# Values projected with tokens on the partitions, and score keys taken by image columns, in two attention blocks

## The chip, the cores and the metric

The kernel runs on one core of one Trainium2 chip. The metric is device time in microseconds (us): the median of several executions of the whole program. Beside it stands one profiled execution, from which every duration of a single instruction below is taken. A core has five engines that run side by side: TensorE (PE) multiplies matrices, VectorE (DVE), ScalarE (ACT) and GpSimd (POOL) work on elements, and SyncE (SP) here only issues transfers. They wait for each other through semaphores.

## What is computed

The reference applies two layers to four images of 32 x 32 tokens with 768 channels, in float32. Each layer is `x = x + attention(groupnorm(x))`, the norm having 32 groups and no weights. Cut to what matters:

```python
qkv = x @ Wqkv                      # layer 1: x @ qkv_w.T + qkv_b
q, k, v = 12 heads of 64 channels each
rel_h = einsum('bhwc,hkc->bhwk', q, Rh)   # one number per query and key row
rel_w = einsum('bhwc,wkc->bhwk', q, Rw)   # one number per query and key column
scores = scale * q @ k.T + (rel_h[..., :, None] + rel_w[..., None, :])
out = softmax(scores) @ v
return out @ Wproj + bproj
```

In layer 1 q is scaled once more in the score and once in the position terms. The softmax of a query runs over all 1024 keys, so the order in which the keys stand doesn't change it, as long as the values stand in the same order.

## The kernel before, in words

**Units.** An "image" in the code is one image in one layer, so there are 8 (`NI`), and each has 6 pairs of heads (`NP`); a pair fills 128 partitions, 64 channels for each head. There are 48 pairs, `g`. The queries of a pair come in 8 tiles of 128 (`n`). A unit is one `(g, n)`; the main loop goes through the 384 units, and an image takes its six pairs one after the other.

**Layout.** The normed input `xn` lies with channels on the partitions, in 6 tiles of 128 channels by 1024 tokens. A product with it contracts over channels.

**Projections.** `project_in(g, which, i)` computes q, k or v of a pair (`which` 0, 1, 2) for one half `i` of the tokens. For every tile of 128 channels it issues two matmuls, one for the upper and one for the lower 64 channels, each with its own PSUM bank; the two occupy different rows of the array. The weights are stationary and the tokens move, 512 at a time, so the result has channels on the partitions. The two banks are added on the way out: ACT copies the first (L234, or L236 with the bias in layer 1), DVE adds the second (L237). It is a generator with six steps of two matmuls.

**Values.** For q and k the result stays as it is. For v it is written with tokens reordered, element by element 16 bytes apart, into a temporary, and then `turn_values` (L249) transposes it on TensorE in eight 128 x 128 blocks (L254) and ACT copies it out (L255), so that tokens are on the partitions. Each of the eight blocks is a "plane" of 128 keys.

**Positions.** `positions(g, i)` multiplies half of the queries with the table of relative positions, copies the result into a temporary (L274) and writes it to HBM from ACT's queue (L276). `diagonals(g)` reads it back with slanted access patterns, 16 transfers on SP's queue (L295), into `rel`. `biases` adds the row and the column term into a tile of 128 queries by 1024 keys on POOL (L305).

**Scores.** `scores` multiplies queries and keys (L317), DVE adds the biases and finds the minimum of the negated score (L326), ACT takes the exponential and its sum (L330), and `divide` normalises on POOL (L340). The result lies with queries on the partitions.

**Turning the weights.** `turn` transposes blocks of 32 x 32 on DVE (L354), which puts the second index of a key, its column in the image, on 32 partitions. For two tiles of queries together ("a quarter") the result is written to HBM (L357) and `read_back` fetches it in such a form (L365) that each of eight planes has 128 keys on the partitions. Which keys a plane holds follows from this round trip, and the values must be stored to match. `weigh` multiplies values and planes (L380), both heads side by side in the columns of the array, and DVE copies the result out (L385).

**Output.** `project_out` multiplies with the output weights (L449) in two parts of three pairs each, adds the residual and keeps statistics for the next layer's norm. In layer 0 the statistics of the next image's input come from half chunks that are loaded for this alone (`load_stats`, tile `xs`), as only three of its six chunks (`AHEAD`) are resident at that time.

**Order.** It is written out by hand. In each unit the loop issues what earlier units deferred (the lists `early` and `later`), biases two units ahead, the scores of the next unit, then the turning of the present one, and then a share of the list `todo`, which holds the next pair's projections and four output groups. `shares = [6, 6, 0, 6, 12, 6, 0, 12]` gives the steps for n = 0 to 7. So the next pair's six projection groups are spent by n = 5; at n = 7 there follow output groups, with `turn_values` between them. `weigh` stands at n = 6 for the first two quarters and at n = 2 of the next pair for the others. Deferred work runs one or two units later. Engines take their instructions in this order, and so does each queue: a transfer whose buffer isn't free holds up all those behind it on SP. TensorE's results go to two PSUM tiles of two banks for the scores (`ps_s`) and two for everything else (`ps_m`).

Of the kernel before, what the change touches and what calls it, by code (L numbers as in the profile page):

```python
# [52 lines left out]
def attention_blocks(ctx: ExitStack, tc: tile.TileContext, a: dict, out: bass.AP):  # L55
# [3 lines left out]
    const = ctx.enter_context(tc.tile_pool(name="const", bufs=1))  # L59
    wpool = ctx.enter_context(tc.tile_pool(name="weights", bufs=3))  # L60
    wopool = ctx.enter_context(tc.tile_pool(name="wo", bufs=3))
    xpool = ctx.enter_context(tc.tile_pool(name="x", bufs=NC + AHEAD))
    apool = ctx.enter_context(tc.tile_pool(name="attn", bufs=6))
    qkpool = ctx.enter_context(tc.tile_pool(name="qk", bufs=2))
    vpool = ctx.enter_context(tc.tile_pool(name="v", bufs=2))
    scpool = ctx.enter_context(tc.tile_pool(name="sc", bufs=6))
    tmppool = ctx.enter_context(tc.tile_pool(name="tmp", bufs=2))
    tbpool = ctx.enter_context(tc.tile_pool(name="tb", bufs=3))
    ptpool = ctx.enter_context(tc.tile_pool(name="pt", bufs=2))
    relpool = ctx.enter_context(tc.tile_pool(name="rel", bufs=2))  # L70
    xspool = ctx.enter_context(tc.tile_pool(name="xs", bufs=1))
    iopool = ctx.enter_context(tc.tile_pool(name="io", bufs=4))
# [15 lines left out]

    def load_x(im, c):
        l, b = images[im]  # L90
        x = xpool.tile([P, S], FP, tag="xn", name=f"xn_{im}_{c}")
        xn_of[im].append(x)
        nc.sync.dma_start(out=x, in_=srcs[l][b][c * P : (c + 1) * P, :])

    def load_w(g, which):
        im, pair = divmod(g, NP)
        src = a[f"wqkv{images[im][0]}"][pair].rearrange("k p (c o) -> k p c o", c=NC)
        w = wpool.tile([P, NC, P], FP, tag="w", name=f"w_{g}_{which}")
        w_of[g, which] = w
        nc.sync.dma_start(out=w, in_=src[which])  # L100

# [4 lines left out]


    ident = const.tile([P, P], FP, tag="ident", name="ident")
    make_identity(nc, ident)

# [33 lines left out]
    def stats(im, c, i, x):  # L144
# [5 lines left out]
        if i == 1:  # L150
            nc.vector.bn_aggr(mv_of[im][:, c, :], st.rearrange("p i s -> p (i s)"))

    def load_stats(im, c, i):
        l, b = images[im]
        if c < AHEAD:
            x = xn_of[im][c][:, i * HALF : (i + 1) * HALF]
            later.append(lambda: stats(im, c, i, x))
            return
        x = xspool.tile([P, HALF], FP, tag="xs", name=f"xs_{im}_{c}_{i}")
        nc.sync.dma_start(out=x, in_=srcs[l][b][c * P : (c + 1) * P, i * HALF : (i + 1) * HALF])  # L160
        later.append(lambda: stats(im, c, i, x))

# [42 lines left out]

    qkv_of, v_of, rel_of, t_of = {}, {}, {}, {}

    def project_in(g, which, i):

        im, pair = divmod(g, NP)  # L210
        l = images[im][0]
        xn, w = xn_of[im], w_of[g, which]
        cols = slice(i * HALF, (i + 1) * HALF)
        if i == 0:
            pool, tag = (tmppool, "tmp") if which == 2 else (qkpool, "qk"[which])
            qkv_of[g, which] = pool.tile([P, S], FP, tag=tag, name=f"{'qkv'[which]}_{g}")
        to = qkv_of[g, which][:, cols]
        if which == 2:
            to = qkv_of[g, 2].rearrange("p (k j y) -> p y k j", y=4, k=NT)[:, 2 * i : 2 * i + 2]
        t = ps_m.tile([P, 2, HALF], FP, tag="m", name=f"pj_{g}_{which}_{i}")  # L220
        for c in range(NC):
            for a in range(2):
                rows = slice(a * D, (a + 1) * D)
                nc.tensor.matmul(  # L224
                    t[:, a, :], lhsT=w[rows, c, :], rhs=xn[c][rows, cols],
                    start=(c == 0), stop=(c == NC - 1),
                )
            if c < NC - 1:
                yield True
        t = [t[:, a, :] for a in range(2)]  # L230
        if which == 2:
            t = [x.rearrange("p (y k j) -> p y k j", y=2, k=NT) for x in t]
        if l == 0:
            nc.scalar.copy(to, t[0])  # L234
        else:
            nc.scalar.activation(to, t[0], AF.Identity, bias=bqkv[:, which, pair : pair + 1])  # L236
        nc.vector.tensor_tensor(to, t[1], to, ALU.add)  # L237
        if which == 0:
            (later if g else mid).append(lambda: positions(g, i))
        if which == 2 and i == 1:  # L240
            late.append(lambda: turn_values(g))
        if i == 1 and g + 1 < NPAIR:
            later.append(lambda: load_w(g + 1, which))
        if which == 2 and i == 1 and pair == NP - 1 and im + 1 < NI:
            for c in range(AHEAD, NC):
                load_x(im + 1, c)
        yield True

    def turn_values(g):  # L249

        v_of[g] = vpool.tile([P, NT, P], FP, tag="v", name=f"v_{g}")
        t = ps_m.tile([P, NT, P], FP, tag="m", name=f"vt_{g}")
        for k in range(NT):
            nc.tensor.transpose(t[:, k, :], qkv_of[g, 2][:, k * P : (k + 1) * P], ident)  # L254
        nc.scalar.copy(v_of[g], t)  # L255

    def positions(g, i):

        l = images[g // NP][0]
        q = qkv_of[g, 0]  # L260
        if i == 0:
# [21 lines left out]
    def diagonals(g):  # L283
        td = t_of[g]
        for h in range(2):
            for ax in range(2):
                for y in range(4):


                    at = HW * y * 2 * P + h * P + HW - 1 + 2 * HW * ax - (y if ax == 0 else 0)  # L290
                    src = bass.AP(
                        td.tensor, td.offset + at,
                        [[2 * P - ax, HW], [P * 2 * P - (4 if ax == 0 else 0), NT], [1, HW]],
                    )
                    nc.sync.dma_start(out=rel_of[g][32 * y : 32 * y + 32, h, ax, :, :], in_=src)  # L295

# [3 lines left out]
    def biases(g, n):  # L300
        rel = rel_of[g]
        for h in range(2):
            sc = scpool.tile([P, HW, HW], FP, tag="sc", name=f"sc_{g}_{n}_{h}")
            sc_of[g, n, h] = sc
            nc.gpsimd.tensor_tensor(  # L305
                sc, rel[:, h, 0, n, :].unsqueeze(2).to_broadcast([P, HW, HW]),
                rel[:, h, 1, n, :].unsqueeze(1).to_broadcast([P, HW, HW]), ALU.add,
            )

    def scores(g, n):  # L310
        q, k = qkv_of[g, 0], qkv_of[g, 1]
        ps = [ps_s.tile([P, S], FP, tag="s", name=f"s_{g}_{n}_{h}") for h in range(2)]
# [11 lines left out]
        for h in range(2):  # L324
            sc = sc_of[g, n, h].rearrange("p y x -> p (y x)")
            nc.vector.tensor_tensor_reduce(  # L326
# [8 lines left out]
    def divide(g, n):  # L335
        st = st_of[g, n]
        nc.vector.reciprocal(st[:, 2, :], st[:, 1, :])  # L337
        for h in range(2):
            sc = sc_of[g, n, h].rearrange("p y x -> p (y x)")
            nc.gpsimd.tensor_scalar(sc, sc, st[:, 2, h : h + 1], 1.0, ALU.mult, ALU.mult)  # L340
# [29 lines left out]
    def weigh(g, quarters):  # L370

        if quarters[0] == 0:
            attn_of[g] = apool.tile([P, S], FP, tag="attn", name=f"attn_{g}")
        n = len(quarters)
        av = ps_m.tile([P, S], FP, tag="m", name=f"av_{g}_{quarters[0]}")[:, : n * 2 * P]
        for at, quarter in enumerate(quarters):
# [7 lines left out]
        at = quarters[0] * 2 * P  # L384
        nc.vector.tensor_copy(  # L385
            attn_of[g][:, at : at + n * 2 * P].rearrange("p (q n r i) -> p q r n i", q=n, n=2, r=4),
            av.rearrange("p (q r n i) -> p q r n i", q=n, n=2, r=4),
        )

# [14 lines left out]
    def fetch(upto):  # L404

        while fetched[0] <= min(upto + 2, len(parts) - 1):
            im, p, o, i = parts[fetched[0]]
# [23 lines left out]
    def fetch_last():  # L431
# [3 lines left out]
        for c in range(NC // 2, NC):  # L435
            w = wpool.tile([P, NC, P], FP, tag="w", name=f"w_last_{c}")
            nc.sync.dma_start(out=w, in_=src[c])
            for o in range(NC):
                wo_of[NI - 1, o, c] = w[:, o, :]
# [37 lines left out]

    early, mid, later, late, behind, behind2 = [], [], [], [], [], []

# [4 lines left out]
    def prepare(g):  # L484
        return [(project_in(g, which, i), NC) for which in range(3) for i in range(2)]

# [4 lines left out]
    def take(groups, n):  # L491
# [8 lines left out]
        while groups and groups[0][1] == 0:  # L500
            for _ in groups.pop(0)[0]:
                pass

    with tc.manual_schedule(engines=ENGINES):
# [23 lines left out]
        for at, (g, n) in enumerate(units):  # L528
            im, pair = divmod(g, NP)
            end = im + 1 == NI  # L530
            if n == 0:
                shares = [6, 6, 0, 6, 12, 6, 0, 12]
                ins = (todo if at == 0 else []) + (prepare(g + 1) if g + 1 < NPAIR else [])
                if pair < 3:
# [7 lines left out]
                else:  # L542
                    todo = ins + put_out(im, 0, range(8, 12))
                    if end:
                        fetch_last()
                        todo += put_out(im, 1, range(12)) + put_out(im, 2, range(0, 12, 2))
                        shares = [0, 6, 6, 6, 6, 2, 0, 4]
            if pair < 3 and not end and n % 4 == 0 and 2 * pair + n // 4 < AHEAD:
                load_x(im + 1, 2 * pair + n // 4)
            if pair < 3 and im + 1 < B and n in (1, 3, 5, 6):  # L550
                c, i = divmod(4 * pair + n // 2, 2)
                load_stats(im + 1, (c + AHEAD) % NC, i)
            run(early)
# [12 lines left out]
            if n == NT - 1:  # L566
                take(todo, share // 4)
                share -= share // 4
            if late and n == NT - 1 or at == 1:
                late.pop(0)()  # L570
            turn(g, n)
# [72 lines left out]
```

## Time and profile before

| | us |
|---|---|
| median of three runs | 3561.37 (3557.85 to 3562.34) |
| the profiled execution: its time | 3557.89 |
| the profiled execution: its span, first to last instruction | 3556.0 |
| TensorE busy in the span | 3511.2 |
| VectorE busy | 2404.5 |
| GpSimd busy | 2298.1 |
| ScalarE busy | 1309.4 |
| TensorE weight loads busy (beside the products) | 1733.6 |

The transfers move 1084 MB, 305 GB/s on the mean. Busy time of an engine is time in which at least one of its instructions was running. In a row of the groups of instructions the line of the code comes first, then the engine, the operation, output and input by their names, shapes, the count, and after the bar the busy time in us and the mean duration of one in ns; last, how long the engine had been idle just before such instructions, and whose end let them go. Matmuls overlap, so their mean duration is longer than the time that one more of them costs. What one costs is read from the chain, where each piece begins as the one before it ends. A row of the stages holds the stretch, its length, and busy time and count for PE, its weight loads, DVE, ACT and POOL, then the granted TensorE clock, the share of the transfer engines and GB/s. In the list of transfers the median time from issue to landing is 6.5 us for the position products, 6.9 us for the weights and 2.1 us for each position read.

### The profile page before, as it was taken

The page shows a single profiled execution, that of the slowest core. Times are in us where ns is not written, and L with a number is a line of the kernel's source. Part 1 is how long each engine was busy: PE and PEld are TensorE (multiplying, and loading weights), DVE is VectorE, ACT ScalarE, POOL GpSimd, SP SyncE. Part 2 cuts the span into 40 slices and gives each one's busy share as a digit, 9 for nine tenths or more (in the row PEclk, how much of TensorE's full clock was granted, in tenths as well). Part 3 has the DMA queues.
Part 4 walks back from the last instruction along what each step waited for, and adds up shares of the span by engine and source line. Part 5 has one row for each costly group of instructions (what it writes and reads, how often), then busy time and mean ns, then how long its engine had stood idle before and what let it go on. Part 6 is the DMA issues. An engine that isn't in the chain of part 4 may idle for free.

```text
span 3556.0 us, 51176 instructions
## 1 busy us (share of the span) xinstructions
PE 3511.2 (99%) x19200; PEld 1733.6 (49%) x19200; DVE 2404.5 (68%) x3533; ACT 1309.4 (37%) x1992; POOL 2298.1 (65%) x1548
## 2 busy tenths in 40 slices
PE   6999999999999999999999999999999999999998
PEld 3455545454544445454444445454444445454443
DVE  3776767767677676666766667666766667666666
ACT  2444333333333333333334343333334343333331
POOL 2777666666666666666666666666666666666663
PEclk9999999999999999999999999999999999999999
DMA  3989988888988888988988888988889888888876
GB/s 126 322 310 314 327 300 323 315 311 301 328 322 309 312 305 313 321 309 287 325 318 320 308 289 321 324 317 285 314 320 327 308 289 318 315 311 281 311 278 261
DMA packets 629593, 1084.29 MB, mean 305 GB/s; under 512 B 247648, under 2 KB 310624, under 8 KB 580192
## 3 DMA queue, kind: packets, MB, share of 16 engines
q1 hardware_dynamic: 577600, 1028.58, 82.3%
q10 hardware_dynamic: 51744, 52.44, 4.2%
q8 instruction: 151, 2.47, 0.3%
q14 instruction: 98, 0.80, 0.1%
HBM read 580.59 MB, written 500.27 MB: 304 GB/s over the span
## 4 chain that ended last, share of the span: by engine, by line
PE 96%; DMA 2%; DVE 1%; POOL 1%; issue 0%; SPq 0%; ACT 0%; DVEq 0%; POOLq 0%
PE pj L224 41%; PE s L317 19%; PE av L380 19%; PE o L449 14%; PE tp L269 3%; PE vt L254 1%; DMA td<-tb 0%; DVE sc L326 0%; DVE tb L354 0%; POOL sc L305 0%; DMA w<-in_wqkv 0%; DMA xs<-in_x 0%; POOL sc L340 0%; SPq L295 0%; DMA pt<-td 0%
## 5 line engine op out<-in xcount | busy, mean ns | idle before, releaser
L340 POOL TENSOR_SCALAR sc<-sc,sm 128x1024 f32<-128x1024 f32 x768 | 851.7, 1122 | 1167.8 <-DVE sm L337 1136.1
L224 PE MATMUL pj<-xn,w 64*128 64x512 f32 x6912 | 1537.1, 591 | 27.1 <-DVE xn L199 26.0
L305 POOL TENSOR_TENSOR sc<-rel 128x1024 f32<-128x1024 f32 x768 | 1458.1, 1920 | 42.3 <-DMA rel<-tdr 42.3
L330 ACT ACTIVATE sc<-sc,sm 128x1024 f32<-128x1024 f32 x768 | 879.2, 1145 | 1427.8 <-DVE sm L326 1427.8
L326 DVE CUSTOM_DVE_ANT_0 sc<-s,sc 128x1024 f32<-128x1024 f32 x768 | 909.8, 1222 | 291.9 <-PE s L317 277.7
L224 PEld LDWEIGHTS pj<-xn,w 64*128 64x128 f32 x6912 | 674.8, 188 | 843.1 <-issue 813.3
L354 DVE STREAM_TRANSPOSE tb<-sc 128x1024 f32<-128x1024 f32 x768 | 909.4, 1222 | 3.6 <-DMA td<-tb 2.9
L317 PE MATMUL s<-k,q 64*128 64x512 f32 x3072 | 752.1, 598 | 7.4 <-DVE sm L326 7.3
L380 PE MATMUL av<-pt,v 128*64 128x256 f32 x6144 | 685.7, 381 | 2.3 <-DMA pt<-td 2.1
L380 PEld LDWEIGHTS av<-pt,v 128*64 128x64 f32 x6144 | 433.0, 137 | 284.6 <-issue 29.6
L449 PE MATMUL o<-attn,wo 128*128 128x512 f32 x1080 | 487.5, 601 | 0.0
L317 PEld LDWEIGHTS s<-k,q 64*128 64x128 f32 x3072 | 288.3, 187 | 340.7 <-issue 321.4
L449 PEld LDWEIGHTS o<-attn,wo 128*128 128x128 f32 x1080 | 197.8, 190 | 258.1 <-issue 247.3
L237 DVE TENSOR_TENSOR v<-pj,v 128x512 f32<-128x512 f32 x96 | 108.2, 1127 | 285.7 <-ACT v L234 141.4
L385 DVE COPY attn<-av 128x512 f32<-128x512 f32 (+1 forms) x97 | 66.3, 684 | 179.5 <-PE av L380 179.5
L274 ACT COPY t<-tp 128x1024 f32<-128x1024 f32 x96 | 97.2, 1012 | 216.5 <-PE tp L269 216.3
L330 ACT ACTIVATION_READ_ACCUMULATOR sc<-sc,sm 128x1 f32 x768 | 143.1, 186 | 0.0
L237 DVE TENSOR_TENSOR q<-pj,q 128x512 f32<-128x512 f32 x96 | 66.4, 692 | 109.9 <-ACT q L234 59.5
L237 DVE TENSOR_TENSOR k<-pj,k 128x512 f32<-128x512 f32 x96 | 66.2, 689 | 92.5 <-ACT k L234 46.8
L269 PEld LDWEIGHTS tp<-tab,q 64*128 64x128 f32 x1536 | 99.2, 187 | 40.6 <-issue 40.1
L460 DVE SCALAR_TENSOR_TENSOR res<-o,bo,res 128x512 f32<-128x512 f32 x84 | 62.9, 749 | 70.1 <-PE o L449 59.1
L269 PE MATMUL tp<-tab,q 64*128 64x128 f32 x1536 | 108.1, 278 | 0.0
(38 smaller groups left out, 810.1 us busy)
## 6 DMA issues: line engine op xcount, KB each, us to landing
td<-tb SPq DMA_DIRECT2D x384, 1024.0 KB, 5.6
pt<-td SPq DMA_DIRECT2D x382, 1024.0 KB, 7.8
w<-in_wqkv SPq DMA_DIRECT2D x144, 384.0 KB, 6.9
tdr<-t ACTq DMA_DIRECT2D x96, 512.0 KB, 6.5
rel<-tdr SPq DMA_DIRECT2D x768, 32.0 KB, 2.1
part<-res SPq DMA_DIRECT2D x84, 256.0 KB, 5.5
res<-part SPq DMA_DIRECT2D x84, 256.0 KB, 8.8
wo<-in_wo SPq DMA_DIRECT2D x90, 192.0 KB, 8.4
```

The costliest lines, as they stand in the source:

```text
L224: nc.tensor.matmul(t[:, a, :], lhsT=w[rows, c, :], rhs=xn[c][rows, cols], start=(c == 0), stop=(c == NC - 1),)
L237: nc.vector.tensor_tensor(to, t[1], to, ALU.add)
L269: nc.tensor.matmul(ps[:, h, j, :], lhsT=q[rows, at * P : (at + 1) * P], rhs=tabs[l][rows, :], start=True, stop=True,)
L274: nc.scalar.copy(t, ps.rearrange("p h j r -> p j h r"))
L305: nc.gpsimd.tensor_tensor(sc, rel[:, h, 0, n, :].unsqueeze(2).to_broadcast([P, HW, HW]), rel[:, h, 1, n, :].unsqueeze(1).to_broadcast([P, ...
L317: nc.tensor.matmul(ps[h][:, cols], lhsT=q[rows, n * P : (n + 1) * P], rhs=k[rows, cols], start=True, stop=True,)
L326: nc.vector.tensor_tensor_reduce(out=sc, in0=ps[h], in1=sc, scale=-scale, scalar=BIG, op0=ALU.add, op1=ALU.min, accum_out=st[:, 0, h : h + 1],
L330: nc.scalar.activation(sc, sc, AF.Exp, bias=st[:, 0, h : h + 1], scale=-1.0, accum_out=st[:, 1, h : h + 1],)
L340: nc.gpsimd.tensor_scalar(sc, sc, st[:, 2, h : h + 1], 1.0, ALU.mult, ALU.mult)
L354: nc.vector.transpose(tb[:, :, j, :], sc_of[g, n, h])
L380: nc.tensor.matmul(av[rows, at * 2 * P : (at + 1) * 2 * P], lhsT=v_of[g][:, k, rows], rhs=pt_of[g, quarter, h][:, :, k, :], start=(k == 0) ...
L449: nc.tensor.matmul(t, lhsT=wo_of[im, o, c], rhs=attn_of[im * NP + c][:, cols], start=(c == c0), stop=(c == c1 - 1),)
```

## The change

Values are projected for two pairs, that is four heads, at once by a new function `project_values`. In it the tokens are stationary and the weights move: for each plane of 128 tokens and each half tile of channels, 128 columns of `xn` are loaded into the array and 256 value channels stream through. The result has tokens on the partitions. There are no transposes of v, no temporary for it, and no identity matrix. A plane is every eighth token, so the 128 stationary columns lie 8 floats apart in `xn`.

So that planes of scores hold the same tokens, keys are stored by image columns (`k` is written in the order x, y), and the biases are added in that order. The round trip through HBM is as it was; what it puts into plane k is now every eighth token. The groups of v of two pairs are spread over both: groups 0 and 1 are issued with the first pair's q and k, groups 2 and 3 with the second's. The value bias of layer 1 is added to the weighted sum in `weigh`, since the weights of a query sum to one.

Value weights come as one transfer of 768 KB for two pairs into a single buffer of their own. The other weights have two buffers instead of three, output weights two instead of three and are fetched two parts later, the temporary one instead of two, v three instead of two. The tile `xs` is gone: for the statistics, whole chunks go through the three resident input tiles first, and the chunks that stay there are loaded a pair later. For the first pair, half of the position reads are issued by ACT.

```diff
-    wpool = ctx.enter_context(tc.tile_pool(name="weights", bufs=3))
-    wopool = ctx.enter_context(tc.tile_pool(name="wo", bufs=3))
+    wpool = ctx.enter_context(tc.tile_pool(name="weights", bufs=2))
+    wopool = ctx.enter_context(tc.tile_pool(name="wo", bufs=2))
-    vpool = ctx.enter_context(tc.tile_pool(name="v", bufs=2))
+    vpool = ctx.enter_context(tc.tile_pool(name="v", bufs=3))
-    tmppool = ctx.enter_context(tc.tile_pool(name="tmp", bufs=2))
+    tmppool = ctx.enter_context(tc.tile_pool(name="tmp", bufs=1))
-    xspool = ctx.enter_context(tc.tile_pool(name="xs", bufs=1))
...
+        if which == 2:
+            w = wpool.tile([P, NC, 2 * P], FP, tag="wv", bufs=1, name=f"wv_{g}")
+            src = a[f"wv{images[im][0]}"][pair // 2]
...
-        if which == 2:
-            to = qkv_of[g, 2].rearrange("p (k j y) -> p y k j", y=4, k=NT)[:, 2 * i : 2 * i + 2]
...
+        if which == 1:
+            to = to.rearrange("p (x y) -> p x y", x=HW)[:, :, i * HW // 2 : (i + 1) * HW // 2]
+            t = [x.rearrange("p (y x) -> p x y", x=HW) for x in t]
...
-    def turn_values(g):
-
-        v_of[g] = vpool.tile([P, NT, P], FP, tag="v", name=f"v_{g}")
-        t = ps_m.tile([P, NT, P], FP, tag="m", name=f"vt_{g}")
-        for k in range(NT):
-            nc.tensor.transpose(t[:, k, :], qkv_of[g, 2][:, k * P : (k + 1) * P], ident)
-        nc.scalar.copy(v_of[g], t)
+    def project_values(g, i):
+
+        im, pair = divmod(g, NP)
+        xn, w = xn_of[im], w_of[g, 2]
+        if i == 0:
+            for h in range(2):
+                v_of[g + h] = vpool.tile([P, NT, P], FP, tag="v", name=f"v_{g + h}")
+        t = ps_m.tile([P, 2, 2, 2 * P], FP, tag="m", name=f"pv_{g}_{i}")
+        for k in range(2):
+            for c in range(NC):
+                for a in range(2):
+                    rows = slice(a * D, (a + 1) * D)
+                    nc.tensor.matmul(
+                        t[:, a, k, :],
+                        lhsT=xn[c][rows, :].rearrange("p (m k) -> p k m", k=NT)[:, 2 * i + k, :],
+                        rhs=w[rows, c, :], start=(c == 0), stop=(c == NC - 1),
+                    )
+                if c % 2 and (k, c) != (1, NC - 1):
+                    yield True
+        for h in range(2):
+            to = v_of[g + h][:, 2 * i : 2 * i + 2, :]
+            cols = slice(h * P, (h + 1) * P)
+            nc.scalar.copy(to, t[:, 0, :, cols])
+            nc.vector.tensor_tensor(to, t[:, 1, :, cols], to, ALU.add)
+        if i == 3:
+            if g + 2 < NPAIR:
+                later.append(lambda: load_w(g + 2, 2))
+            if pair == NP - 2 and im + 1 < NI:
+                for c in range(AHEAD, NC):
+                    load_x(im + 1, c)
+        yield True
...
-                    nc.sync.dma_start(out=rel_of[g][32 * y : 32 * y + 32, h, ax, :, :], in_=src)
+                    (nc.scalar if h and not g else nc.sync).dma_start(out=rel_of[g][32 * y : 32 * y + 32, h, ax, :, :], in_=src)
...
-                sc, rel[:, h, 0, n, :].unsqueeze(2).to_broadcast([P, HW, HW]),
-                rel[:, h, 1, n, :].unsqueeze(1).to_broadcast([P, HW, HW]), ALU.add,
+                sc, rel[:, h, 1, n, :].unsqueeze(2).to_broadcast([P, HW, HW]),
+                rel[:, h, 0, n, :].unsqueeze(1).to_broadcast([P, HW, HW]), ALU.add,
...
+        if images[im][0] == 0:
+            nc.vector.tensor_copy(to, av)
+        else:
+            for q in range(n):
+                nc.vector.tensor_scalar(to[:, q], av[:, q], bqkv[:, 2, pair : pair + 1], None, ALU.add)
...
-        while fetched[0] <= min(upto + 2, len(parts) - 1):
+        while fetched[0] <= min(upto, len(parts) - 1):
...
-        return [(project_in(g, which, i), NC) for which in range(3) for i in range(2)]
+
+        todo = [(project_in(g, which, i), NC) for which in range(2) for i in range(2) if g < NPAIR]
+        if g % 2:
+            return todo + [(project_values(g - 1, i), NC) for i in (2, 3)]
+        return todo + [(project_values(g, i), NC) for i in (0, 1) if g < NPAIR]
...
+    loads = {(1, 0): 0, (1, 4): 1, (2, 0): 2}
+    loads0 = {(0, 0): 0, (0, 1): 1, (0, 4): 2}
...
-            if pair < 3 and not end and n % 4 == 0 and 2 * pair + n // 4 < AHEAD:
-                load_x(im + 1, 2 * pair + n // 4)
-            if pair < 3 and im + 1 < B and n in (1, 3, 5, 6):
-                c, i = divmod(4 * pair + n // 2, 2)
-                load_stats(im + 1, (c + AHEAD) % NC, i)
+            if (pair, n) in loads and not end:
+                load_x(im + 1, loads[pair, n])
+            if im + 1 < B:
+                if (pair, n) in loads0:
+                    load_x(im + 1, loads0[pair, n], loads0[pair, n] + AHEAD)
+                if pair < 3 and n in (1, 3, 5, 6):
+                    c, i = divmod(4 * pair + n // 2, 2)
+                    x = xn_of[im + 1][c % AHEAD][:, i * HALF : (i + 1) * HALF]
+                    later.append(lambda c=c, i=i, x=x: stats(im + 1, (c + AHEAD) % NC, i, x))
...
-            if late and n == NT - 1 or at == 1:
-                late.pop(0)()
```

## The prediction

> **What bounds the kernel.** I read the page first, then the groups kept apart by shape, the stages, and the chain that ended last within one pair of heads.
>
> ```profile
> span 3556.0 us, 51176 instructions
> ...
> PE 3511.2 (99%) x19200; PEld 1733.6 (49%) x19200; DVE 2404.5 (68%) x3533; ACT 1309.4 (37%) x1992; POOL 2298.1 (65%) x1548
> ...
> PE 96%; DMA 2%; DVE 1%; POOL 1%; issue 0%; SPq 0%; ACT 0%; DVEq 0%; POOLq 0%
> PE pj L224 41%; PE s L317 19%; PE av L380 19%; PE o L449 14%; PE tp L269 3%; PE vt L254 1%; DMA td<-tb 0%; DVE sc L326 0%; DVE tb L354 0%; POOL sc L305 0%; DMA w<-in_wqkv 0%; DMA xs<-in_x 0%; POOL sc L340 0%; SPq L295 0%; DMA pt<-td 0%
> ```
>
> TensorE is busy and is the chain; every other engine has at least 30% to spare. The stages say where this holds.
>
> ```profile
> 0.00:90.00 90.00, 60.39 (x294) 28.24 (x296) 33.44 (x61) 19.64 (x27) 27.12 (x28) 0.96 0.39 126
> 208.00:3490.00 3282.00, 3279.95 (x18054) 1624.96 (x18052) 2246.44 (x3286) 1231.00 (x1873) 2170.02 (x1452) 1.00 0.88 310
> ```
>
> From 208 to 3490 us TensorE is idle for 2.05 us (second figure against the first). So in the 48 pairs of heads what is taken off TensorE's own stream is gained in full, and what is added is lost in full. One pair takes 72.69 us (the projection run that starts at 1023.56 starts again at 1096.25). Its pieces in the chain, as start, length, what:
>
> ```profile
> 1023.56 10.30 PE pj L224 x48
> ...
> 1035.58 5.15 PE pj L224 x24
> ...
> 1042.45 7.06 PE av L380 x64
> ...
> 1051.42 2.77 PE o L449 x6
> 1054.19 0.87 PE vt L254 x8
> 1055.07 7.90 PE o L449 x18
> ...
> 1076.90 0.89 PE tp L269 x16
> ```
>
> These give the prices. Two 64-row products of 512 columns run side by side: 5.15/12 = 0.429 us. Two products of 256 columns (av, side by side in columns): 7.06/32 = 0.221. Two 64-row products of 128 columns (tp): 0.89/8 = 0.111. So time goes by columns, and a pair of 128-column weight loads fits under 0.111 us.
>
> [...]loads are busy 49%, and the tp pairs above leave no gap. [...] The new stationary operand takes every eighth float, 32 bytes apart[...]. No operand of TensorE is read so in this trace, but the value evacuation writes floats 16 bytes apart, and there it shows on two engines:
>
> ```profile
> L237 DVE TENSOR_TENSOR v<-pj,v 128x512 f32<-128x512 f32 x96 | 108.2, 1127 | 285.7 <-ACT v L234 141.4 <-ACT v L236 139.3 <-DMA rel<-tdr 5.0
> L237 DVE TENSOR_TENSOR q<-pj,q 128x512 f32<-128x512 f32 x96 | 66.4, 692 | 109.9 <-ACT q L234 59.5 <-ACT q L236 50.5
> L234 ACT COPY v<-pj 128x512 f32<-128x512 f32 x48 | 53.1, 1106 | 135.0 <-PE pj L224 135.0
> L234 ACT COPY q<-pj 128x512 f32<-128x512 f32 x48 | 28.1, 586 | 84.9 <-PE pj L224 84.9
> L380 PEld LDWEIGHTS av<-pt,v 128*64 128x64 f32 x6144 | 433.0, 137 | 284.6 <-issue 29.6 <-ACT v L236 18.2 <-ACT v L234 17.4
> L224 PEld LDWEIGHTS pj<-xn,w 64*128 64x128 f32 x6912 | 674.8, 188 | 843.1 <-issue 813.3 <-DVE xn L199 26.5 <-DVE tb L354 1.6
> ```
>
> Stepped against packed, 512 elements cost ACT 520 ns and DVE 435 ns more, about 0.85 to 1.0 ns an element. Packed weights cost (188 - 137)/64 = 0.80 ns a column (the last two rows).
>
> **Part by part.**
>
> Transposes out. 8 of them take 0.87 us of the chain in each pair (the three lines of o, vt, o; the products around them are of the same 128-row shape, so no change of shape goes with them). 48 x 0.87 = 41.8 us gained. The ACT copies of 47.5 us in all and the stepped value evacuation go too, but lie under TensorE.
>
> Value products. Before, a pair had 12 side-by-side couples of 512 columns, 12 x 0.429 = 5.15 us. After, two pairs share 48 couples of 256, so 24 a pair. If the loads hide: 24 x 0.221 = 5.30, 0.15 more, 48 x 0.15 = 7.4 us lost (from tp and pj in proportion it would be 3). Do the loads hide? Bounds for one stepped load of 128 columns: below, 0.107 us as packed (128 x 0.83), which leaves the 34 us gain whole. Doubled, [...]128 x 1.67 = 0.213 us: still under 0.221, but only just. With the measured stepped element of DVE or ACT, about 1.85 to 1.90 ns: 0.24 us, then the load sets the pace and 24 x 0.243 = 5.83 costs 0.68 a pair, leaving 0.19 x 48 = 9 us of gain. Above: if the float is fetched in two passes and each is doubled, 0.427 us, 24 x 0.431 = 10.34, 5.19 more a pair, 249 us in all. I take 0.213: the doubling is what both other engines show, and I see no evidence of a second pass. The gain is lost at (5.15 + 0.87)/24 = 0.251 us a couple.
>
> Value evacuation. Eight ACT copies and eight DVE adds of 256 packed elements for two pairs, about 0.37 us (586 less 256 x 0.83) and 0.42 (the 256-column attn copy took 424 ns). For the even pair of a couple the last group ends at n = 5 and weigh reads it at n = 6, behind only the 1.72 us of the next scores. ACT, DVE, DVE in line is 0.05 + 0.37 + 0.42 + 0.42 = 1.3 us, and in the trace DVE waits at that point 1.2 us for ACT, so it is free. Hidden with 0.4 us to spare; with the cover gone it costs at most about 0.5 us in 24 pairs, 12 us.
>
> Keys by columns. ACT and DVE write k in runs of 16 and read the product stepped; [...]I allow what v paid: 1106 and 1127 ns instead of 586 and 689, 4 instructions a pair, 1.0 us on ACT and 0.9 on DVE. Keys are done at n = 4, read at n = 7: hidden under TensorE. v's own stepped 2.25 us of DVE a pair leaves. Biases, exponentials, block transposes, the plane round trip: same shapes, same counts, nothing.
>
> Value bias. In layer 1 two adds of 256 (0.42 each) for one copy of 512 (0.69), 0.16 us of DVE more per weigh; hidden, since the tile is next read five units later at the earliest.
>
> Queues and buffers. Bytes are the same; a value weight is one transfer of 768 KB per two pairs on one buffer, reloaded after n = 5 and used again four units of 9 us later, against 6.9 us of landing. q and k weights keep one buffer each, as they had in effect. Output weights come two parts later, still a pair ahead of use. One temporary instead of two: ACT's second position copy must wait until the first has been read out. From the first write's issue (1078.88) to the second copy (1087.71) are 8.8 us, the write lands in 6.5 us median, 12.1 at most, so now and then ACT stands up to 3.3 us, with exponentials queued behind, which DVE and POOL want next; ACT has 4.4 us idle just before. Nothing for TensorE. On SP the half-chunk loads for statistics become three whole chunks issued earlier, past nothing that is late.
>
> Start. 384 KB more of value weights stand before the gather of the statistics: 4.33 MB landed between 0.7 and 14.3 us, some 320 GB/s, so 1.2 us later. Against it, half of the 16 position reads (0.49 us of SP each) go to ACT's queue, so the second bias, which starts at 60.56, can start at 58.9; and the wait for the half-chunk (DVE 4.2 us at 120, after which TensorE is idle 2.0 us) goes, since that chunk comes earlier. TensorE's half-clock windows after those two stalls (65 to 69, 136 to 140 us) may go as well. What is late next: ACT queues the last key copy behind its eight issues, 53.05 to about 55.0, still ahead of the scores at 57.98. Between 2 us lost and 8 gained; I take 4 gained.
>
> Sum: 41.8 - 7.4 + 4 = 38.4 us. The profiled execution took 3557.89 (span 3556.0 and 1.9 around it), so 3519.5; it was 3.5 under the median of the runs, so 3523.
>
> **Rivals.**
>
> 1. Loads at 0.24 us set the pace of the value products: gain 9 plus 4 of the start, 3549. For it: ACT's and DVE's stepped elements cost 1.85 to 1.90 ns though their packed rates differ (0.83, 1.04), as if the memory and not the engine set it. Against it: those rows hold fixed parts that I can't separate.
>
> 2. Two-pass loads at 0.43 us: 3561 + 249 - 42 - 4 = 3764, slower. Place: the 24 couples of each pair; it decides from 0.251 us on. For it: a packed column costs 0.80 ns where the transpose's load, 141 ns for 128 columns, fits half that, so an ordinary load may go over its columns twice. [...] Intermediate loads of 0.26 to 0.35 us give 3570 to 3660.
>
> 3. The loads hide but a new wait eats the gain: values late for weigh (12 us), ACT held by the single temporary: 3535 to 3550. Against it: the margins above.
>
> **Chances.** Forecast (loads hide) 0.60, 3510 to 3535. Rivals 1 and 3 together 0.16, 3535 to 3562. Rival 2 0.22, of it two-pass 0.16. The rest, 0.02, is faster still. A measurement tells 0.2%, 7 us, from no change: same is 3554 to 3568. Faster 0.60 + 0.02 + 0.10 = 0.72, same 0.05, slower 0.23. To leave out no more than 0.2 the range runs to 3600.
>
> **What would show it.** Right: no vt row; the value products at 0.217 to 0.222 us a couple with weight loads near 300 ns in their row; a pair of heads at 71.97 us (72.69 - 0.87 + 0.15). Rival 1: the couples at 0.24 to 0.25, loads back to back. Rival 2: loads above 450 ns and TensorE waiting between products. Rival 3: couples at 0.22, and weigh's first product waiting on DVE. [...]

## The result and the profile after

The changed kernel takes 3566.78 us (median of 4 runs, 3564.07 to 3567.03), the kernel before 3559.61 in the same comparison: a ratio of 1.002, interval 1.0003 to 1.0038. It is slower by a fifth of a per cent, where 3523 and a gain were forecast. The profiled executions have spans of 3565.2 and 3556.0 us.

The page of the changed kernel, its parts on busy time and on the chain that ended last:

```profile
span 3565.2 us, 55101 instructions
...
PE 3515.4 (99%) x21120; PEld 2044.5 (57%) x21120; DVE 2381.5 (67%) x3676; ACT 1226.5 (34%) x2040; POOL 2297.6 (64%) x1546
...
PE 96%; DMA 2%; DVE 1%; issue 0%; SPq 0%; ACT 0%; POOL 0%; DVEq 0%; ACTq 0%
PE pj L213 28%; PE s L328 19%; PE av L394 19%; PE pv L248 15%; PE o L470 14%; PE tp L280 3%; DMA tdr<-t 1%; DMA pt<-td 0%; DMA td<-tb 0%; DMA wv<-in_wv 0%; DVE tb L365 0%; SPq L306 0%; DVE sc L337 0%; DMA per<-mv 0%; SPq L94 0%
```

TensorE is still busy for 99% of the span and still the chain. The transposes are out of it, and `pv`, the new value products, holds 15%, where a third of `pj`'s 41% would be 14%. Its groups, products and weight loads, and the loads of the other projections, by shape:

```profile
L248 PEld LDWEIGHTS pv<-wv,xn 64*128 64x128 f32 x4608 | 570.2, 331 | 31.1 <-DVE v L259 9.9 <-issue 9.6 <-DVE tb L365 1.6
L248 PE MATMUL pv<-wv,xn 64*128 64x256 f32 x4608 | 567.8, 398 | 0.0
L213 PEld LDWEIGHTS pj<-xn,w 64*128 64x128 f32 x4608 | 453.8, 188 | 568.7 <-issue 534.2 <-DVE xn L192 27.9 <-ACT t L285 2.1
```

Two things can be read here. A load of 128 stepped floats lasts 331 ns against 188 packed, and its group is busy as long as the products are (570.2 and 567.8): the loads run back to back. And there are 4608 records of each kind. The code calls 2304 products, so each float32 call is recorded as two matmuls and two loads.

The chain of one pair of heads, start, length and what:

```profile
1024.14 5.15 PE pj L213 x24
1029.29 5.73 PE pv L248 x48
...
1036.73 5.73 PE pv L248 x48
...
1053.15 10.50 PE o L470 x24
...
1080.20 7.06 PE av L394 x64
...
1096.93 5.15 PE pj L213 x24
```

Two value groups of 5.73 us (24 side-by-side couples of records each, 5.73/24 = 0.2388 us a couple) stand where there were two of 5.15: 1.16 us more a pair. The output products are one run of 10.50 where they were 2.77, 0.87 and 7.90 with the transposes between: 1.04 us less.

When the first score product of a unit starts, read from both traces, gives the balance by stage (us):

| from, to (pair, n) | before | after | difference |
|---|---|---|---|
| start to (2, 0) | 194.66 | 193.37 | -1.29 |
| (2, 0) to (4, 0), in the first image | 127.55 | 129.86 | +2.32 |
| (4, 0) to (47, 0), 43 pairs | 3126.84 | 3130.11 | +3.27 |
| (47, 0) to the end | 106.98 | 111.90 | +4.92 |

The sum is +9.22, the difference of the spans. From 330 to 3400 us TensorE has no gap in either kernel (busy for 3070.00 of 3070.00 us), so the row of the 43 pairs shows the steady price.

### The profile page after: what moved, and what is told of

Its sections match the earlier page's. It is cut to its first block, busy times and chain, and to the rows that moved or that the text cites. A ratio compares the mean times of both kernels' runs of the same rounds, so it can differ in the third digit from the quotient of the medians.

```text
span 3565.2 us, 55101 instructions
## 1 busy us (share of the span) xinstructions
PE 3515.4 (99%) x21120; PEld 2044.5 (57%) x21120; DVE 2381.5 (67%) x3676; ACT 1226.5 (34%) x2040; POOL 2297.6 (64%) x1546
## 4 chain that ended last, share of the span: by engine, by line
PE 96%; DMA 2%; DVE 1%; issue 0%; SPq 0%; ACT 0%; POOL 0%; DVEq 0%; ACTq 0%
PE pj L213 28%; PE s L328 19%; PE av L394 19%; PE pv L248 15%; PE o L470 14%; PE tp L280 3%; DMA tdr<-t 1%; DMA pt<-td 0%; DMA td<-tb 0%; DMA wv<-in_wv 0%; DVE tb L365 0%; SPq L306 0%; DVE sc L337 0%; DMA per<-mv 0%; SPq L94 0%
## 5 line engine op out<-in xcount | busy, mean ns | idle before, releaser
L213 PE MATMUL pj<-xn,w 64*128 64x512 f32 x4608 | 1031.1, 591 | 29.7 <-DVE xn L192 27.4
L213 PEld LDWEIGHTS pj<-xn,w 64*128 64x128 f32 x4608 | 453.8, 188 | 568.7 <-issue 534.2
L248 PEld LDWEIGHTS pv<-wv,xn 64*128 64x128 f32 x4608 | 570.2, 331 | 31.1 <-DVE v L259 9.9
L248 PE MATMUL pv<-wv,xn 64*128 64x256 f32 x4608 | 567.8, 398 | 0.0
L470 PE MATMUL o<-attn,wo 128*128 128x512 f32 x1080 | 477.3, 598 | 0.0
L328 PEld LDWEIGHTS s<-k,q 64*128 64x128 f32 x3072 | 299.4, 188 | 291.3 <-issue 264.7
L259 DVE TENSOR_TENSOR v<-pv,v 128x256 f32<-128x256 f32 x192 | 81.5, 424 | 320.3 <-ACT v L258 320.3
L258 ACT COPY v<-pv 128x256 f32<-128x256 f32 x192 | 71.4, 372 | 380.6 <-PE pv L248 333.0
L285 ACT COPY t<-tp 128x1024 f32<-128x1024 f32 x96 | 97.2, 1012 | 249.2 <-PE tp L280 147.5
```

The lines of the kernel that those rows point to most:

```text
L213: nc.tensor.matmul(t[:, a, :], lhsT=w[rows, c, :], rhs=xn[c][rows, cols], start=(c == 0), stop=(c == NC - 1),)
L248: nc.tensor.matmul(t[:, a, k, :], lhsT=xn[c][rows, :].rearrange("p (m k) -> p k m", k=NT)[:, 2 * i + k, :], rhs=w[rows, c, :], start=(c == ...
L328: nc.tensor.matmul(ps[h][:, cols], lhsT=q[rows, n * P : (n + 1) * P], rhs=k[rows, cols], start=True, stop=True,)
L470: nc.tensor.matmul(t, lhsT=wo_of[im, o, c], rhs=attn_of[im * NP + c][:, cols], start=(c == c0), stop=(c == c1 - 1),)
```

## The experiments

The question was what sets 0.2388 us. **Theory:** the load of 128 stepped floats, 331 ns where a packed one lasts 188. **Rival:** products of 256 columns and 64 rows run so by themselves. The first kernel still computes the whole function: its planes are 128 neighbouring tokens, so that nothing is stepped for TensorE, and keys and biases are reordered to match.

**Packed planes, keys reordered to match.**

```diff
-            to = to.rearrange("p (x y) -> p x y", x=HW)[:, :, i * HW // 2 : (i + 1) * HW // 2]
-            t = [x.rearrange("p (y x) -> p x y", x=HW) for x in t]
+            to = to.rearrange("p (q k b) -> p q k b", q=4, k=NT)[:, :, 4 * i : 4 * i + 4, :]
+            t = [x.rearrange("p (k b q) -> p q k b", q=4, k=4) for x in t]
...
-                        lhsT=xn[c][rows, :].rearrange("p (m k) -> p k m", k=NT)[:, 2 * i + k, :],
+                        lhsT=xn[c][rows, (2 * i + k) * P : (2 * i + k + 1) * P],
...
-                sc, rel[:, h, 1, n, :].unsqueeze(2).to_broadcast([P, HW, HW]),
-                rel[:, h, 0, n, :].unsqueeze(1).to_broadcast([P, HW, HW]), ALU.add,
+                sc.rearrange("p (q k) (e f) -> p q (k e) f", q=4, e=4),
+                rel[:, h, 1, n, :].rearrange("p (f q) -> p q f", q=4).unsqueeze(2).to_broadcast([P, 4, HW, 8]),
+                rel[:, h, 0, n, :].unsqueeze(1).unsqueeze(3).to_broadcast([P, 4, HW, 8]), ALU.add,
```

> The changed kernel with planes of 128 neighbouring tokens, so that the stationary operand of the value products is read packed; keys are stored so that position 32*(8q+k)+b holds token 128k+4b+q, and the biases are added in that order, which makes GpSimd read the column term 16 bytes apart. Theory (a load of 128 floats, [...]takes 0.239 us and sets the pace of the value products): the couple of two records falls from 0.239 to 0.217-0.221 us, weight loads from 331 to about 188 ns, 48 x 48 couples x 0.018-0.022 = 41 to 50 us less than the changed kernel, about 3517 to 3526. Rival (products of 256 columns with 64 rows run at 0.239 whatever their load): same time as the changed kernel, about 3567. If GpSimd's stepped read is slow, its bias rises from 1.92 us to up to 2.9, hidden at 3.0 ms busy.

**Only the load packed, or stepped by two or four floats.** Three kernels with one line changed, the first of them shown; the other two take every second token of a block of 256, and every fourth of a block of 512. In these three the values do not match the planes; they are there for the time alone:

```diff
-                        lhsT=xn[c][rows, :].rearrange("p (m k) -> p k m", k=NT)[:, 2 * i + k, :],
+                        lhsT=xn[c][rows, (2 * i + k) * P : (2 * i + k + 1) * P],
```

> The changed kernel with only the stationary operand of the value products read packed (tokens of a block instead of every eighth; the values then do not match the planes, so the attention output is another one). Theory: couples at 0.217-0.221 us, 3517 to 3526. Rival (256-column products at 0.239 by themselves): 3567.

> As the one before, with every second token (8 bytes apart[...]; values do not match the planes). [...]hidden under the product: couples at 0.217-0.221, 3517 to 3526. Rival (any step makes the load slow): couples at 0.239, 3567.

> As the one before, with every fourth token (16 bytes apart[...]; values do not match the planes). [...]0.239 us a couple as with every eighth, 3567. Rival (the price rises with the distance): between 0.221 and 0.239, 3530 to 3560.

Measured:

| floats apart | mean load, ns | a couple, us | (4, 0) to (47, 0), us | time, us |
|---|---|---|---|---|
| 1 (load alone) | 187 | 5.18/24 = 0.2158 | 3082.88 | 3517.41 (one run) |
| 1 (whole kernel) | 187 | 0.2158 | 3082.88 | 3518.96 (4 runs), ratio to the kernel before 0.9887, interval 0.987 to 0.9903 |
| 2 | 193 | 0.2158 | 3082.88 | 3516.09 (one run) |
| 4 | 324 | 5.58/24 = 0.2325 | 3117.50 | 3552.32 (one run) |
| 8 (the change) | 331 | 0.2388 | 3130.11 | 3566.78 (4 runs) |

The loads and products with the load alone packed, and one value group in the chain:

```profile
L248 PE MATMUL pv<-wv,xn 64*128 64x256 f32 x4608 | 514.1, 376 | 0.0
L248 PEld LDWEIGHTS pv<-wv,xn 64*128 64x128 f32 x4608 | 446.9, 187 | 91.7 <-issue 32.0 <-DVE v L259 11.1 <-DVE tb L365 1.6
...
1019.40 5.18 PE pv L248 x48
```

The loads of two and of four floats apart, the latter with its value group:

```profile
L248 PEld LDWEIGHTS pv<-wv,xn 64*128 64x128 f32 x4608 | 460.0, 193 | 79.1 <-issue 31.5 <-DVE v L259 11.1 <-DVE tb L365 1.6
```

```profile
L248 PEld LDWEIGHTS pv<-wv,xn 64*128 64x128 f32 x4608 | 554.1, 324 | 33.2 <-DVE v L259 10.9 <-issue 9.4 <-DVE tb L365 1.6
...
1027.98 5.58 PE pv L248 x48
```

The rival falls: the same product with a packed load takes 0.2158, and its loads are busy for 446.9 of the products' 514.1 us, so they no longer fill the time. The load sets the pace when it is stepped by four or eight floats (loads busy for 554.1 and 570.2 us, products for 552.9 and 567.8). Packed loads give back 47.2 us in the 43 pairs (3130.11 - 3082.88), which is 2 x (5.73 - 5.18) x 43; in the times of the two kernels it is 49 (3566.78 - 3517.41).

The fourth run did not come out as the theory had it. It forecast 0.239 and 3567, the same price for every fourth token as for every eighth, which was an estimate of mine; 0.2325 and 3552 lie in the range of its rival, that the price rises with the distance. But the rise is no even one: from one float to two the mean load grows by 6 ns, from two to four by 131, from four to eight by 7. So most of the price comes between 8 and 16 bytes; why it comes there was not shown, and the small rise beyond, 12.6 us in the 43 pairs, stays unexplained. A step of three floats wasn't run.

In the whole kernel, GpSimd's biases now read one operand 16 bytes apart, in runs of eight. The row of that kernel and of the changed one:

```profile
L316 POOL TENSOR_TENSOR sc<-rel 128x1024 f32<-128x1024 f32 x768 | 1889.0, 2483 | 41.8 <-DMA rel<-tdr 41.8
```

```profile
L316 POOL TENSOR_TENSOR sc<-rel 128x1024 f32<-128x1024 f32 x768 | 1457.0, 1918 | 40.9 <-DMA rel<-tdr 40.9
```

They cost 432 us more of GpSimd, and the 43 pairs take 3082.88 us as with the load alone packed: hidden, as expected.

**The transposes by themselves,** taken out of the kernel before:

```diff
-        t = ps_m.tile([P, NT, P], FP, tag="m", name=f"vt_{g}")
-        for k in range(NT):
-            nc.tensor.transpose(t[:, k, :], qkv_of[g, 2][:, k * P : (k + 1) * P], ident)
-        nc.scalar.copy(v_of[g], t)
+        nc.scalar.copy(v_of[g], qkv_of[g, 2].rearrange("p (k c) -> p k c", k=NT))
```

> The kernel before without the eight transposes of a pair: the values are copied out as they are, so the attention output is another one. Theory (the transposes cost 0.87 us of TensorE and 0.17 more by breaking up the output products, in the 45 pairs that are bound by TensorE, not in the first three): 1.04 x 45 = 47 us less than the kernel before, 3512. Rival (0.87 alone in all 48): 42 us less, 3517. Rival 2 (the projected values then end on another wait): less than 30.

It took 3511.75 us (one run) against 3559.19, 47.4 less, as the theory said. In its chain the output products are one piece again:

```profile
1039.94 10.50 PE o L446 x24
```

From (4, 0) to (47, 0) it gained 46.5 us, 1.08 a pair. From (2, 0) to (4, 0) it gained nothing: 129.24 us against 127.55 before. There, with no output products at n = 7, TensorE must wait until DVE has read earlier scores, and the transposes only filled part of that wait. The first of two such places (start, length, what, idle before), in the kernel before and in the changed one:

```profile
196.58 1.09 PE L254 MATMUL vt<-ident,v 128*128 128x128 f32 x8
198.08 2.27 PE L317 MATMUL s<-k,q 64*128 64x512 f32 x6 [0.41 <-DVE sm L326]
```

```profile
196.79 2.70 PE L328 MATMUL s<-k,q 64*128 64x512 f32 x7 [1.43 <-DVE sm L337]
```

Without transposes TensorE is idle 1.43 us twice in this stretch, in this kernel as in the changed one. The 1.7 us that this kernel took longer fit one stretch of 3.4 us at half clock, which its trace records at 260.9 us (its price is worked out below).

**The single temporary.** In the changed kernel ACT's copy of position products waits for the write before it. Two of ACT's waits in it, in us in total, times and the longest:

```profile
ACT t L285 <- PE tp L280: 147.5, 71, 4.7
...
ACT t L285 <- DMA tdr<-t: 99.7, 16, 8.6
```

and the first of them in order of time on ACT (start, length, what, idle before and its releaser):

```profile
86.06 0.43 ACTq L287 DMA_DIRECT2D tdr<-t  x1
...
97.94 1.01 ACT L285 COPY t<-tp 128x1024 f32<-128x1024 f32 x1 [7.80 <-DMA tdr<-t]
98.98 0.38 ACTq L287 DMA_DIRECT2D tdr<-t  x1
99.42 1.15 ACT L341 ACTIVATE sc<-sc,sm 128x1024 f32<-128x1024 f32 x1 [0.46 <-ACT t L285]
```

The next experiment copies in halves, through three temporaries of half the size, otherwise the changed kernel:

```diff
-    tmppool = ctx.enter_context(tc.tile_pool(name="tmp", bufs=1))
+    tmppool = ctx.enter_context(tc.tile_pool(name="tmp", bufs=3))
...
-        t = tmppool.tile([P, 4, 2, P], FP, tag="tmp", name=f"t_{g}_{i}")
-        nc.scalar.copy(t, ps.rearrange("p h j r -> p j h r"))
...
+        for y in range(2):
+            t = tmppool.tile([P, 2, 2, P], FP, tag="tmp", name=f"t_{g}_{i}_{y}")
+            nc.scalar.copy(t, ps[:, :, 2 * y : 2 * y + 2, :].rearrange("p h j r -> p j h r"))
...
```

> The changed kernel with the position products copied and written in two halves through three temporaries of half the size, so that no copy has to wait for a write before it. Theory (in the steady part ACT's 100 us of waiting for the write of the single temporary lie beside TensorE, and only the first ones count): waits on that write fall from 16 to none or nearly none, time 3 us lower than the changed kernel at most, 3562 to 3567; the lead over the kernel before of 3.0 us that the changed kernel has at the fourth unit stays until the eighth. Rival (ACT held up delays the scores everywhere): 10 us or more lower.

The waits for this write fall from 99.7 us to 1.5, and the time is 3562.89 us (one run). The lead over the kernel before, 3.4 us at the fourth unit, is 2.2 at the eighth; it doesn't stay whole, as was expected, but in the changed kernel it was lost altogether. The second pair starts 3.84 us earlier than in the changed kernel (124.60 against 128.44), and that distance is the same at pair 47; the 43 pairs take 3130.11 us in both. So the waits cost nearly 4 us, all in the first pair, and nothing where TensorE is the bound. The run changes the number of buffers and the size of the copies together; which of the two it takes was not tried.

**The split of the first position reads over two queues,** undone in the kernel with packed planes:

```diff
-                    (nc.scalar if h and not g else nc.sync).dma_start(out=rel_of[g][32 * y : 32 * y + 32, h, ax, :, :], in_=src)
+                    nc.sync.dma_start(out=rel_of[g][32 * y : 32 * y + 32, h, ax, :, :], in_=src)
```

> Packed planes with all position reads of the first pair on SP's queue, as in the kernel before. Theory (the split over two queues lets the second bias start 1.7 us earlier, at the price of a later key copy): the second and third unit start 1 to 3 us later than with the split; the time at most 3 us higher, 3519 to 3522. Rival (the split gains nothing): same unit starts within 0.5 us.

The second and third unit start 0.4 and 0.8 us earlier without the split (61.95 against 62.38, 78.10 against 78.93), where the theory had 1 to 3 us later. Here the split gains nothing. But the five kernels with the split whose biases are not slowed spread over 2.4 us at the second unit (60.84 to 63.26), and GpSimd's first bias takes 2.4 us in this kernel, so that the second could hardly start sooner (61.28 without the split). What the split is worth in the changed kernel, with biases of 1.9 us, was not tried. The time, 3514.82 us (one run) against 3518.96, says nothing of it: the two traces record 6.8 and 20.5 us at half clock.

**A version that beats both.** Packed planes, three half temporaries, and the first value weights loaded after the statistics:

```diff
-    for which in range(3):
+    for which in range(2):
         load_w(0, which)
...
         for n in sorted(stages):
             stages[n]()
+        load_w(0, 2)
```

> Packed planes of 128 neighbouring tokens, the three half temporaries, and the first value weights loaded only after the statistics have been spread. Theory: the 3519 us of the packed planes less 1.3 us at the start (weights ahead of the statistics) and up to 3 (waits for the temporary): 3513 to 3519. Rival (start and end hang on when TensorE's half clock falls): 3519 +/- 4, no difference that can be told.

3512.69 us (4 runs, 3506.94 to 3517.03), ratio 0.9864, interval 0.9847 to 0.988. Against packed planes alone, 0.9887 with an interval of 0.987 to 0.9903, the gain of 6 us is not shown: the intervals overlap, the two were taken in different comparisons, and packed planes without the split took 3514.82. Pair 4 starts 4.6 us earlier in it (321.00 against 325.64), the end of the profiled one only 2.6; its trace has 23.9 us at half clock. The 43 pairs take 3082.88 us in both.

## Why the prediction was wrong

**The step that failed is the value products,** in two terms.

The count. "48 couples of 256, so 24 a pair" counts calls of the code, but 0.221 us and 0.429 us are prices of records, and there are two records for each float32 call. The page before had it: 6912 records of `pj` are 144 a pair, where the code calls 72. With the right count, packed loads at the forecast's own price give 48 x 0.221 - 24 x 0.429 = +0.31 us a pair, not +0.15, and the forecast would have been 7.7 us higher, 3531. The point at which the gain is lost moves from 0.251 to (10.30 + 0.87)/48 = 0.233 us a couple. My second rival's guess from the load times, that a load goes over its columns twice, was not shown: each call is recorded with two loads of 128, but in both kernels, so that adds nothing by itself.

The price. I took 0.213 us for a stepped load, hidden under 0.221: an estimate, twice the packed 0.107, as ACT's and DVE's stepped instructions took 1106 and 1127 ns against 586 and 692 packed. It was 0.2388, which is 1.87 ns a float, the stepped element that ACT and DVE showed in the trace before (1.85 to 1.90 ns). My first rival had just this price and this sign, couples at 0.24 with loads back to back, and argued from the two engines' like prices that the memory, not the engine, sets it, which was not shown; with the wrong count it promised a gain of 9 us (3548 by its own sum, not 3549), with the right one it loses. In the runs a load stepped by two floats is as good as free (193 ns against 187, both at 0.2158 us a couple), and by four or eight it costs 1.82 or 1.87 ns a column (0.2325 and 0.2388 us over 128).

Neither term alone turns the gain into a loss. The right count at the forecast's price costs 0.31 us a pair, the right price at the wrong count 24 x 0.2388 - 5.15 = 0.58. Both together cost 1.16, more than the 0.87 of the transposes. The price is the larger term.

**Transposes.** 41.8 us were forecast, 47.4 measured: 0.17 us a pair more, since they broke the output products in two, and nothing where TensorE had to wait after them in the first image. That a saving is gained in full "in the 48 pairs" was read too widely there. Right in kind, off by an eighth.

**Sum with what was measured:** +1.16 x 48 = 55.7 for the products, -47.4 for the transposes, so +8.3; the medians differ by 7.2. That these agree so well is in part luck, as runs of the kernel before lie up to 8 us apart in one comparison. The stages give the account of the profiled pair.

**The start** was to give 4 us. It gave 1.3 up to pair 2, and the clock is enough to account for that. The clock records of the kernel before show 10.2 us at half clock (0.50 granted) in the first 140 us (62.3 to 69.1 and 134.0 to 137.4, where I had read 65 to 69 and 136 to 140), worth up to 5 us by the price below; the changed kernel has none there. The single temporary took back 3.84. I had put the price of its waits at "nothing for TensorE". That holds in the steady part, though ACT stood longer than the 3.3 us that I allowed: between 330 and 3400 us 13 times, 76.4 us in all, 7.5 at most. It does not hold at the start, where the write took 11.8 us to land.

**From (2, 0) to (4, 0)** the +2.32 us are twice the 1.16 of the value products; the transposes' time became waiting. **In the 43 pairs** it is 1.16 - 1.08, 0.08 us a pair.

**The end** is 4.9 us longer, which no step foresaw. Between two units of the last pair the same instructions took longer after the same idle time of 1.41 us; TensorE before and after (start, length, what, idle before):

```profile
3465.97 3.13 PE L317 MATMUL s<-k,q 64*128 64x512 f32 x8 [1.41 <-DVE sm L326]
3469.03 5.42 PE L449 MATMUL o<-attn,wo 128*128 128x512 f32 x12
```

```profile
3469.16 4.92 PE L328 MATMUL s<-k,q 64*128 64x512 f32 x8 [1.41 <-DVE sm L337]
3474.01 6.94 PE L470 MATMUL o<-attn,wo 128*128 128x512 f32 x12
```

By the trace's clock records TensorE ran at half its clock (0.5 granted) for 6.8 us here, and for 3.4 more at 3535 us; the kernel before has no such stretch at its end. What one costs can be read from (2, 0) to (4, 0) in the kernels with packed planes, where TensorE's instructions are the same and it is idle 1.43 us twice in each: 127.67 us without any (split undone), 129.36 with one of 3.4 us (at 264.9), 131.06 with two (the version that beats both, at 195.2 and 260.1). So where TensorE is busy 3.4 us at half clock cost 1.7, and 10.2 would cost 5.1, an estimate in proportion. In both profiled executions there are 10.2, at the start in one and at the end in the other, so the account by stages has about 5 us that moved. Why the same stall is followed by half clock in one execution and not in another was not tried.

**What held.** Value evacuation is hidden, with more to spare than I had allowed. In the pair where weigh comes next, the value products end at 1115.26 us, ACT's first copy starts at 1115.31, DVE's first add ends at 1116.13, and weigh's first product starts at 1116.90, 0.77 us later; it is 0.77 or 0.78 in all 24 such pairs. The second copy, which waits for the first add, writes the values of the next pair, so that the four do not stand in line before weigh, as I had summed them. Queues, single weight buffers, biases and the value bias cost TensorE nothing: from 330 to 3400 us it is busy without a gap in both kernels. Writing keys by columns cost nothing at all, where I had allowed the 1106 and 1127 ns of v's stepped evacuation, as an estimate:

```profile
L226 ACT COPY k<-pj 128x512 f32<-128x512 f32 x48 | 28.0, 584 | 61.3 <-PE pj L213 53.9 <-DMA rel<-tdr 7.4
L229 DVE TENSOR_TENSOR k<-pj,k 128x512 f32<-128x512 f32 x96 | 66.1, 689 | 92.8 <-ACT k L226 46.7 <-ACT k L228 46.1
```

These read the product 128 bytes apart and write runs of 16 floats, in 584 and 689 ns; the kernel before, with packed keys, took 586 and 689.

## What to carry to other kernels

Before a price from a trace is multiplied, bring both to one unit: count the records of a row, divide by the calls of the code, and use the same kind on both sides. Where a stationary operand is stepped by 16 or 32 bytes (loads of 324 and 331 ns here, against 187 packed), compare its load with the time between products, as well as the product. And a layout that must be stepped somewhere is best stepped where an engine has room: here the keys' evacuation and GpSimd's biases took it for nothing (copies of 584 and adds of 689 ns, against 586 and 689 before; biases of 2.48 us instead of 1.92 with the 43 pairs at 3082.88 us either way), where TensorE paid 47 us in 43 pairs.

## What was not expected of the hardware

- In float32 a stationary operand of TensorE stepped by two floats loads as good as packed (193 against 187 ns, both 0.2158 us a couple), by four it does not (324 ns, 0.2325 us).
- A stepped float costs about the same on three engines: 1.82 and 1.87 ns a column in TensorE's loads (16 and 32 bytes apart), and 1.85 to 1.90 ns an element in ACT's and DVE's writes (16 bytes apart), though packed they take 0.8 to 1.0. (For ACT, copies of 512 and 1024 packed floats take 586 and 1012 ns, 0.83 an element and 160 fixed; DVE's of 256 and 512 take 424 and 692.)
- ACT and DVE read the product's memory 128 bytes apart (the change, 584 and 689 ns) or 16 bytes apart (packed planes, 584 and 692 ns) as fast as packed (586 and 689 ns); only the step in the other memory showed (v's writes 16 bytes apart, 1106 and 1127 ns).
- GpSimd took 2.48 us instead of 1.92 for a bias with one operand 16 bytes apart, 29% more, not double.
- Eight transposes cost 1.04 us, of which 0.17 are in the products around them, and nothing where TensorE waits next: from (2, 0) to (4, 0) 129.24 us without them and 127.55 with them.
- A stall of 1.4 us is followed by 3.4 or 6.8 us at half clock (0.5 granted) in some executions and by none in others; 3.4 us cost 1.7.
